# A two-layer graph network on one core: the second pass over the adjacency put in one written order, a third chunk of nodes summed by lists, and the nodes' own scores moved into layer 1

## The chip, the cores and the metric

The kernel runs on one core of a Trainium2 chip. TensorE (PE) multiplies matrices, VectorE (DVE) and ScalarE (ACT) work on elements, GpSimd (POOL) issues the indirect gathers here, SyncE (SP) issues most plain DMA transfers, and ACT issues a few. The metric is the device time of one execution in microseconds (us). The profile is of one further execution of the same program.

## The reference, cut to what matters

There are 3327 nodes with 512 features. `adj` is square, mostly zero, with non-zero weights from 0.05 to 1; the probability of an edge falls with the node numbers, so the first nodes (the hubs) have most edges. Cut from the reference:

```
# layer 0
h = relu(layernorm(x))
x = x + adj @ (relu(adj @ (h @ W1) + b1) @ W2) + b2        # W1: 512x128, W2: 128x512
# layer 1
h = relu(layernorm(x))
attn_a = sigmoid(concat([adj @ h, h]) @ Wa.T + ba)          # attn_b likewise with Wb, bb
hs = h @ W_sa
scores = (hs @ a_left)[:, None] + (hs @ a_right)[None, :]
e = where(adj != 0, exp(-leaky_relu(scores, 0.01)), 0)
x_a = (e / (sum(e, axis=1) + 1e-5)) @ hs
x_b = adj @ (h @ W_gcnb) + b_gcnb
x = x + sigmoid(attn_a * x_a + attn_b * x_b)
```

So layer 0 multiplies by `adj` twice, and layer 1 needs for every node the sum of its neighbours' rows of h, once weighted by `adj` and once by `e`. For every node it also needs a left score, a right score, and two logits from the node's own row (the part of Wa and Wb that meets h itself).

## The kernel before, in words

The nodes are padded to 3328 and cut into 26 blocks of 128. `adjT` is the transposed adjacency in DRAM. A chunk is 512 of its columns (one 256 wide); an adj tile is 128 rows by one chunk, 256 KB. All products are in float32, and each takes two passes of PE. The framework that the kernel is written in puts the semaphores in and plans the order of each engine's instructions by priority and readiness in its own model; `queued(...)` and `tc.issue_after(...)` put an instruction behind another one on the same engine, and `tc.high_priority()` moves work forward.

**Pass 1** (lines 541 to 596). Seven chunks from the last columns to the first. For each chunk and each block j, SP loads an adj tile (line 271, eight buffers), PE adds `u[j]` times the tile into `acc_u` (line 568; u is h @ W1, made beside the first chunk, line 333), and DVE takes for each row the maximum over each group of 32 columns (`most`, line 572). From these maxima DVE and PE make lists (lines 452 to 532): for a block of 128 nodes and each group of 32 columns, which rows of `adjT` are non-zero there. `list_rooms` gives each block its room, in steps of 64 rows per group: 0 for block 0, then 8, 7, 6, 5, 5, six times 4, then 3. For the blocks in `OWN` one more step holds the block's own diagonal part, which needs no list. POOL gathers the listed pieces of `adjT` into `ae` (line 166), paced by PE. ACT stores `g`, the relu of the sums, and between chunks loads weights and the columns of block 0 (`a_hub`, five pieces).

**Pass 2** (lines 806 to 860). The product `adj @ g`. For all nodes but the last two chunks it is dense: five chunks, 26 tiles each, line 825. For the last two chunks (blocks 18 to 25, `LISTED = 2`) the rows of g are gathered by list (`g_row`, line 166) and multiplied with the pieces in `ae` (`acc_s`, line 784, 64x32 pieces, four side by side). Each finished chunk gives a generator, `make_h1`, which is stepped between the dense products: for each block it loads x, adds b2, multiplies by W2 (`px`, line 663), adds (line 666), stores x1, normalises (`bn_stats`, `Sqrt`, line 234 to 244), takes the right and left score (line 623), the own logits (line 630, of the blocks that are neither in `OWN` nor in `LATE`), and stores the row of h (line 637). At the end of a chunk PE transposes the left scores (`pl`, line 687). Also stepped here are `make_e_hub` (the masked exponentials of block 0, lines 249 to 256) and `add_hubs` (block 0's two sums over all 26 blocks, `acc_hub`, line 709), and further gathers of `ae`. How often each is stepped is in conditions on the loop counters and in the table `SUMS`.

**Layer 1** (lines 914 to 1138). Block 0 has its sums already. The blocks 25 down to 1 follow. For each: POOL gathers the listed rows of h (`hr` or `rows`, line 166), DVE and ACT make the masked exponentials (`attend`), PE adds the rows by `adj` and by `e` (`sums`, line 981), transposes the result (`turn`, line 995; DVE copies it out, line 1010), multiplies by the weights (`weigh`, lines 1035 and 1042) and adds up the exponentials (`add_up`, line 1018); `finish` (lines 875 to 900) combines these and SP stores the output. In PE's order one round is: weigh an earlier block, turn the block before, add up, sums of this block. For a block in `OWN` its own rows of h are loaded (`h_own`, line 935, three buffers) and its own logits are made here; for the three blocks in `LATE` they are made at the start of layer 1.

Of the kernel before, what the change touches and what calls it, by code (L numbers as in the profile page):

```python
# [18 lines left out]
P = 128  # L19
# [9 lines left out]
LISTED = 2  # L29
LN_EPS = 1e-5  # L30
SUM_EPS = 1e-5
# [7 lines left out]
LATE = 10, 11, 16  # L39

OWN = 1, 6, 7, 8, 12, 13, 14, 15, 17, 18


def list_rooms(n_blocks):

    rooms = [0, 8, 7, 6, 5, 5] + 6 * [4]
    return (rooms + n_blocks * [3])[:n_blocks]
# [3 lines left out]
def kernel(  # L51
# [29 lines left out]
    made_order = []  # L81
    for k, c in enumerate(dense_chunks):
        for c0, w in (c, *listed_chunks[k : k + 1]):
            made_order += range(c0 // P, (c0 + w) // P)
# [3 lines left out]
    extra = [int(i in OWN) for i in range(NB)]  # L88
# [29 lines left out]
    bab_row = kept([P, 2], "bab_row")  # L118
    w_own = kept([P, 2, D], "w_own")
# [20 lines left out]
    def segments(i):  # L140

        r = rooms[i] + extra[i]
        n = -(-r // SEG)
        cuts = [-(-r * k // n) for k in range(n + 1)]
        return list(zip(cuts, cuts[1:]))
# [50 lines left out]
    def load_own(i):  # L196

        n = segments(i)[0][1]
        for h in range(2):
            rows = slice(i * P + h * HALF, i * P + (h + 1) * HALF)  # L200
            nc.scalar.dma_start(
                ae[i][h * HALF : (h + 1) * HALF, 0 : n + 1 : n, :GW],
                adjT[rows, rows].rearrange("j (q i) -> j q i", i=GW),
            )
# [41 lines left out]

    def masked_exp(e, adj):
# [11 lines left out]
    with (  # L259
        tc.tile_pool(name="l0", bufs=1) as l0,  # L260
        tc.tile_pool(name="l0w", bufs=2) as l0w,
        tc.tile_pool(name="adjp", bufs=8) as adjp,
    ):

        def load_adj(j, c, name, n=1):

            c0, w = c
            t = adjp.tile([P, CW], F32, tag="adj", name=f"{name}_{c0}_{j}")
# [17 lines left out]
        HUB_LOADS = 5  # L286

        def load_hub(k):
            rows = slice(k * NB // HUB_LOADS * P, (k + 1) * NB // HUB_LOADS * P)
            nc.scalar.dma_start(  # L290
                a_hub[:, k * NB // HUB_LOADS : (k + 1) * NB // HUB_LOADS, :],
                adjT[rows, :P].rearrange("(j p) i -> p j i", p=P),
            )

        def load_weights():
# [3 lines left out]
            nc.scalar.dma_start(w_own, w_self.partition_broadcast(P))  # L299
            nc.scalar.dma_start(bab_row, b_ab.partition_broadcast(P))  # L300
# [73 lines left out]
        def make_constants():  # L374
# [36 lines left out]
            for r in sorted(set(rooms[1:])):  # L411
                i0, n = rooms.index(r), rooms.count(r)
# [9 lines left out]
                )  # L422
            yield
# [9 lines left out]
        def make_lists(nth, most):  # L433
# [10 lines left out]
            for b in range(w // P):  # L444
                if extra[c0 // P + b]:
                    groups = slice(b * NQ, (b + 1) * NQ)
                    own = flag[:, groups, c0 // P + b]
                    nc.vector.tensor_tensor(own, own, apart, ALU.mult)

# [99 lines left out]
        for n, c in enumerate(back):  # L549
            c0, w = c  # L550
            acc = bank(psA, f"acc_u_{c0}")
            per = CW // w
            most = l0w.tile([P, MG, NB], F32, tag="most", name=f"most_{c0}")
            for j in range(NB):
# [9 lines left out]
                if j % per == 0:  # L564
                    with queued(x_loaded[min(j + 4, NB - 1)] if n == 0 else None):
                        tile_a = load_adj(j, c, "a1", per)
                a = tile_a[:, j % per, :]
                added = nc.tensor.matmul(  # L568
                    acc[:, :w], u[j], a[:, :w], start=(j == 0), stop=(j == NB - 1)
                )  # L570
                with queued(scaled[min(j + 3, NB - 1)] if n == 0 else None):
                    nc.vector.tensor_reduce(  # L572
                        most[:, : w // GW, j], a[:, :w].rearrange("p (b i) -> p b i", i=GW),
                        axis=AX.X, op=ALU.max, apply_absolute_value=True,
                    )
# [11 lines left out]
            with tc.issue_after(chunk_end.ins):  # L587
                if n == 1:
                    load_weights()
                if 0 < n <= HUB_LOADS:  # L590
                    load_hub(n - 1)
                for i in OWN:
                    if n and c0 <= i * P < c0 + w:
                        load_own(i)
# [24 lines left out]
        acc_hub = [bank(psA, f"acc_hub_{k}") for k in range(2)]  # L619

# [6 lines left out]
        def own_logits(i, h, junk):  # L627

            for s in range(2):
# [692 lines left out]
```

## Time and profile before

| | us |
|---|---|
| three runs, median | 825.4 (823.3 to 828.0) |
| profiled execution | 834.5 |
| its span on the core | 832.8 |
| PE busy | 735.6 (88%) |
| DVE busy | 506.0 (61%) |
| POOL busy | 461.1 (55%) |
| ACT busy | 194.5 (23%) |

185.1 MB went through DMA, 222 GB/s over the span. The stages, by the first and last instructions in the trace: pass 1 to 236 us, dense products and the hubs' products to 469, the first blocks of layer 1 to 490, then one block after another.

In the rows of the profile, a group is a line of the kernel, an engine, an operation and its tiles, with count and mean time. The chain is the work that ended last, followed back: each piece has a start, a length, and an engine with a line, or what was waited for. "Another core or an unknown queue" is a wait whose releaser the trace does not show; on one core it is no other core. "Issue" is time in which an engine waited for nothing that is shown. The granted clock is the share of full clock that PE had.

### The profile page before, as it was taken

The numbers are of one execution on the slowest core, as the hardware profiler recorded it, in microseconds if no ns is written. First come the engines' busy times: TensorE is split into PE (matmuls) and PEld (weight loads), VectorE is DVE, ScalarE is ACT, GpSimd is POOL, SyncE is SP. The second block draws the span as 40 slices with busy tenths as digits, with TensorE's granted clock in tenths as the row PEclk, the third lists the DMA queues.
The fourth block names the chain that finished last, engine by engine and source line by source line (L and its number), as shares of the span: only waits on it lengthen the run. The fifth ranks groups of instructions, "written<-read, shape, count | busy, mean of one in ns | idle before, by whom it ended". The sixth has DMA issues, their size and how long they took to land.

```text
span 832.8 us, 11907 instructions
## 1 busy us (share of the span) xinstructions
PE 735.6 (88%) x3595; PEld 404.5 (49%) x3595; DVE 506.0 (61%) x1625; ACT 194.5 (23%) x402; POOL 461.1 (55%) x490
## 2 busy tenths in 40 slices
PE   9999888989899771999899749967999999999995
PEld 7774333444543220444355236633656655665554
DVE  7778868898860611798987225523665557553552
ACT  7770000000000110354544002211212222221121
POOL 2201756766657776534456766674657666767500
PEclk9999989999999875999999969996999999999999
DMA  8788988988878844789994755664667877767510
GB/s 271 245 287 259 326 246 242 293 272 246 232 232 284 262 132 134 240 279 312 327 314 135 241 150 145 199 185 115 195 211 244 255 206 233 240 205 234 178 51 29
DMA packets 104889, 185.08 MB, mean 222 GB/s; under 512 B 18401, under 2 KB 35441, under 8 KB 104818
## 3 DMA queue, kind: packets, MB, share of 16 engines
q1 hardware_dynamic: 66544, 113.43, 41.8%
q0 software_dynamic: 23264, 57.64, 24.3%
q10 hardware_dynamic: 15010, 13.18, 4.9%
q8 instruction: 30, 0.49, 0.2%
q14 instruction: 41, 0.34, 0.1%
HBM read 162.29 MB, written 22.26 MB: 222 GB/s over the span
## 4 chain that ended last, share of the span: by engine, by line
PE 72%; DVE 7%; issue 6%; another core or an unknown queue 6%; DMA 5%; ACT 2%; POOL 1%; SPq 1%; DVEq 0%; ACTq 0%; POOLq 0%
PE acc_u L568 17%; PE acc L981 12%; PE p_b L1035 11%; PE p_a L1042 10%; PE acc_g L825 8%; PE pu L333 3%; PE ptt L995 3%; DMA a<-in_adjT_dram 2%; PE acc_hub L709 2%; PE px L663 2%; PE pt L325 1%; DMA xb<-in_x_dram 1%; PE acc_s L784 1%; DMA hr<-h_rows,row_h 1%
## 5 line engine op out<-in xcount | busy, mean ns | idle before, releaser
L166 POOL DMA_INDIRECT ae<-in_adjT_dram,row_a x194 | 202.6, 1044 | 181.8 <-DVE past L519 54.3
L568 PE MATMUL acc_u<-a,rows 128*128 128x512 f32 (+1 forms) x364 | 161.0, 583 | 0.5 <-DMA a<-in_adjT_dram 0.5
L166 POOL DMA_INDIRECT hr<-h_rows,row_h x120 | 122.7, 1022 | 62.5 <-issue 27.4
L825 PE MATMUL acc_g<-a,g 128*128 128x512 f32 (+1 forms) x260 | 117.1, 584 | 7.2 <-DMA a<-in_adjT_dram 6.8
L572 DVE TENSOR_REDUCE most<-a 128x16 f32<-128x512 f32 (+1 forms) x182 | 112.3, 638 | 11.6 <-issue 6.3
L1035 PE MATMUL p_b<-W_g_sb,tyT 128*128 128x257 f32 x416 | 99.3, 391 | 15.8 <-DVE tyT L1010 15.3
L1035 PEld LDWEIGHTS p_b<-W_g_sb,tyT 128*128 128x128 f32 x416 | 77.8, 192 | 46.5 <-DVE tyT L1010 15.6
L166 POOL DMA_INDIRECT rows<-h_rows,row_h x74 | 75.1, 1015 | 44.3 <-PE acc L981 20.9
L568 PEld LDWEIGHTS acc_u<-a,rows 128*128 128x128 f32 x364 | 67.2, 195 | 58.8 <-issue 56.0
L1042 PE MATMUL p_a<-W_sa_sb,tyT 128*128 128x512 f32 (+2 forms) x216 | 94.2, 577 | 0.2
L1010 DVE COPY tyT<-ptt 128x512 f32<-128x512 f32 x51 | 34.8, 685 | 87.0 <-PE p_a L1042 31.7
L825 PEld LDWEIGHTS acc_g<-a,g 128*128 128x128 f32 x260 | 50.0, 200 | 58.5 <-issue 44.9
L981 PE MATMUL acc<-hr,ae 64*64 64x512 f32 x480 | 68.3, 614 | 4.4 <-issue 4.0
L166 POOL DMA_INDIRECT g_row<-g_rows,row_h x48 | 49.0, 1021 | 20.9 <-issue 13.4
L1042 PEld LDWEIGHTS p_a<-W_sa_sb,tyT 128*128 128x128 f32 x216 | 40.7, 189 | 38.8 <-issue 36.9
L884 ACT ACTIVATE f<-f 128x2 f32<-128x2 f32 x26 | 5.3, 203 | 192.4 <-DVE f L883 97.2
L981 PEld LDWEIGHTS acc<-hr,ae 64*64 64x64 f32 x480 | 27.6, 136 | 33.6 <-issue 33.0
L343 ACT ACTIVATE gT<-acc_u,b_col 128x512 f32<-128x512 f32 (+1 forms) x7 | 4.6, 656 | 163.8 <-DMA a<-in_adjT_dram 90.9
L663 PE MATMUL px<-W_sb,sT 128*128 128x512 f32 x52 | 26.7, 650 | 15.4 <-ACT sT L799 12.0
L666 DVE TENSOR_TENSOR xb<-px,xb 128x512 f32<-128x512 f32 x26 | 17.3, 682 | 36.6 <-PE px L663 28.5
L981 PE MATMUL acc<-rows,ae 64*64 64x512 f32 x296 | 37.1, 593 | 2.5 <-issue 2.3
L623 DVE SCALAR_TENSOR_TENSOR junk<-rows,w_rows 128x512 bf16<-128x512 f32 x52 | 35.6, 684 | 3.2 <-ACT rows L244 1.1
(159 smaller groups left out, 945.2 us busy)
## 6 DMA issues: line engine op xcount, KB each, us to landing
a<-in_adjT_dram SPq DMA_DIRECT2D x286, 256.0 KB
h_rows<-rows SPq DMA_DIRECT2D x26, 260.0 KB
x<-in_x_dram SPq DMA_DIRECT2D x26, 256.0 KB
xb<-in_x_dram SPq DMA_DIRECT2D x26, 256.0 KB
x<-xb ACTq DMA_DIRECT2D x26, 256.0 KB
x1b<-x SPq DMA_DIRECT2D x26, 256.0 KB
out_dram<-va SPq DMA_DIRECT2D x25, 256.0 KB
ae<-in_adjT_dram,row_a POOLq DMA_INDIRECT x194
```

What stands on the lines that cost most here:

```text
L166: return nc.gpsimd.indirect_dma_start(out=dst, out_offset=None, in_=table, in_offset=bass.IndirectOffsetOnAxis(ap=rows, axis=0), bounds_ch ...
L333: nc.tensor.matmul(pu[:, :HID], hT[:, k, :], W1_sb[:, k, :], start=(k == 0), stop=(k == KD - 1))
L568: added = nc.tensor.matmul(acc[:, :w], u[j], a[:, :w], start=(j == 0), stop=(j == NB - 1))
L572: nc.vector.tensor_reduce(most[:, : w // GW, j], a[:, :w].rearrange("p (b i) -> p b i", i=GW), axis=AX.X, op=ALU.max, apply_absolute_value ...
L623: return nc.vector.scalar_tensor_tensor(junk, h, 1.0, w_rows[:, s, :], op0=ALU.mult, op1=ALU.mult, accum_out=into)
L663: last_row[2] = nc.tensor.matmul(px, sT[:, b * P : (b + 1) * P], W2_sb, start=True, stop=True)
L825: added = nc.tensor.matmul(acc[:, :w], g[j], a[:, n % per, :], start=(n == 0), stop=(n == NB - 1))
L981: added = nc.tensor.matmul(taken[i]["acc"][h][q * HALF : (q + 1) * HALF, :], both[half_p, q * n + k, :], taken[i][k0][k][half_p, q, :D], s ...
L995: moved = nc.tensor.transpose(pt[:, k * P : (k + 1) * P], ty[h][:, k * P : (k + 1) * P], ident)
L1010: last = nc.vector.tensor_copy(dst, src)
L1035: nc.tensor.matmul(p_b[n][:, :WH], tyT[:, k, 0, :], W_g_sb[:, k, n * WH : (n + 1) * WH], start=(k == 0), stop=(k == KD - 1),)
L1042: last = nc.tensor.matmul(p_a[:, c0:c1], tyT[:, k, 1, :], W_sa_sb[:, k, c0:c1], start=(k == 0), stop=(k == KD - 1),)
```

## The change

1. Third chunk by lists: `LISTED` is 3, so blocks 14 to 25 are summed by lists in pass 2, and the dense chunks are four (three of 512 and one of 256).
2. One written order for pass 2: the list `PLAN` names each step (d a dense product, s a list block, t the end of a listed chunk, x a block's row, l a transposition of left scores, h a hub product, e the exponentials of the hubs, a a gather of adj pieces), and every PE instruction is put behind the one named before it (`behind_pe`). `MADE` gives the order in which the chunks' rows are made.
3. A row in pass 2: the sum of x1 comes with its addition, the squares, the logarithm and the exponential are taken on ACT (`ln_relu_by_sum`), with one activation table loaded ahead for the whole pass. Only the right score is taken for every block, the left one for block 0 and blocks 22 to 25 (`early`).
4. Layer 1: every block's row is loaded a block ahead (`load_row`), DVE takes the left score (where not early) and the own logits (`own_scores`), PE transposes the left score (`turn_score`) between `add_up` and the next sums. `LATE` is gone; `w_own` and `bab_row` are loaded behind pass 2.
5. adj in pieces of two tiles (512 KB) with six buffers; maxima are taken over both tiles at once except in the first chunk.
6. Block 0's columns are loaded once, as part of the last chunk of pass 1 (in pieces of eight blocks, by SP), and used again in pass 2; products of that chunk are split into block 0's columns and the rest (`product`).
7. Blocks 9, 21 and 24 (`TOP`) have two steps without lists, their own and the 64 first rows of `adjT`, and one step less in lists; a block of five steps is taken in one segment.

```diff
-LISTED = 2
+LISTED = 3
+MADE = "dldlldd"
+PLAN = """
+d25 s1 d3 x1 d3 x1 s1 d2 l1 x1 d1 s1 d2 x1 e2 d5 s1 d2 t1 d2 x1 d2 s1 x1 e2 d6 x1 s1 d3 x1 e2
+d4 s1 d2 x1 l1 h1 s1 x1 e2 h1 t1 h1 a1 h1 d1 a1 d1 x1 a1 h1 s1 h1 x1 a1 e2 h2 a1 d2 a1 d1 s1
...
+d2 a1 h2 x1 a1 h2 a1 x1 h1 a1 h2 a1 h2
+"""
-LATE = 10, 11, 16
-
-OWN = 1, 6, 7, 8, 12, 13, 14, 15, 17, 18
+TOP = 9, 21, 24
+
+OWN = TOP + (1, 6, 7, 8, 12, 13, 14, 15, 17, 18)
...
-    rooms = [0, 8, 7, 6, 5, 5] + 6 * [4]
-    return (rooms + n_blocks * [3])[:n_blocks]
+    rooms = [0, 8, 7, 6, 5, 5, 4, 4, 4, 3, 4, 4] + n_blocks * [3]
+    rooms[21] = rooms[24] = 2
+    return rooms[:n_blocks]
...
-    extra = [int(i in OWN) for i in range(NB)]
+    extra = [int(i in OWN) + int(i in TOP) for i in range(NB)]
...
-        n = -(-r // SEG)
+        n = -(-r // SEG) - (r == SEG + 1)
...
+    def ln_relu_by_sum(dst, src, ln):
+
+        nc.vector.tensor_scalar(ln[:, 1:2], ln[:, 0:1], -1.0 / D, None, op0=ALU.mult)
+        nc.scalar.activation(dst, src, AF.Square, bias=ln[:, 1:2], accum_out=ln[:, 2:3])
+        nc.scalar.activation(ln[:, 3:4], ln[:, 2:3], AF.Ln, bias=eps, scale=1.0 / D)
+        nc.scalar.activation(ln[:, 4:5], ln[:, 3:4], AF.Exp, scale=-0.5)
+        nc.vector.tensor_tensor(ln[:, 0:1], ln[:, 1:2], ln[:, 4:5], ALU.mult)
+        return nc.scalar.activation(dst, src, AF.Relu, bias=ln[:, 0:1], scale=ln[:, 4:5])
...
-        tc.tile_pool(name="adjp", bufs=8) as adjp,
+        tc.tile_pool(name="adjp", bufs=6) as adjp,
...
-            t = adjp.tile([P, CW], F32, tag="adj", name=f"{name}_{c0}_{j}")
+            t = adjp.tile([P, 2 * CW], F32, tag="adj", name=f"{name}_{c0}_{j}")
...
+        def product(acc, w, own, j, a, start, stop):
+
+            hub = w - a.shape[-1]
+            if hub:
+                nc.tensor.matmul(acc[:, :hub], own, a_hub[:, j, :], start=start, stop=False)
+            return nc.tensor.matmul(
+                acc[:, hub:w], own, a, start=start and not hub, stop=stop
             )
...
+            hub = 0 if c0 else P
+            per = 2 * CW // (w - hub)
...
+                        if hub:
+                            load_hub(j, some)
+                        tile_a = load_adj(j, (c0 + hub, w - hub), "a1", some)
...
+                both = some if hub else 2 if n else 1
...
+        with queued(chunk_end):
+            nc.scalar.preload_act_table_set("natural_log_exp_and_others")
...
+        def make_row():
+
+            i = next(made)
+            load_next()
+            x1 = xs.pop(i)
+            assert place[i] - NR < len(e_added)
+            with tc.high_priority():
+                px = bank(psB, f"px_{i}")
+                with behind_pe():
+                    on_pe[0] = last_row[2] = nc.tensor.matmul(
+                        px, sTs.pop(i), W2_sb, start=True, stop=True
+                    )
+                ln = l0w.tile([P, 5], F32, tag="ln5", name=f"ln_b{i}", bufs=3)
+                nc.vector.scalar_tensor_tensor(
+                    x1, px, 1.0, x1, op0=ALU.mult, op1=ALU.add, accum_out=ln[:, 0:1]
+                )
+                nc.scalar.dma_start(x1_dram[i], x1)
+                h = made_row(i)
+                last_row[0] = ln_relu_by_sum(h[:, :D], x1, ln)
+                score(i, h[:, :D], 1, h[:, D : D + 1])
+            last_row[1] = last_row[0]
+            if i in early:
+                last_row[1] = score(i, made_row(i)[:, :D], 0, node[i][:, 0:1])
...
+            while len(unstored) > (0 if place[i] > NB - 7 else 3):
+                store_row(unstored.pop(0))
...
+        plan = [(w[0], int(w[1:])) for w in PLAN.split()]
+        for n in range(4):
+            next(dense)
         gather_g(GR)
...
+        for what, n in plan:
+            for _ in range(n):
+                does[what]()
...
+    with queued(last_row[0]):
+        nc.scalar.preload_act_table(AF.Tanh)
...
+        def load_row(i):
+
+            h_own[i] = h = spw.tile([P, ROW], F32, tag="h_own", name=f"h_own_{i}", bufs=3)
+            nc.sync.dma_start(h, h_dram[i * P : (i + 1) * P, :])
+
+        def own_scores(i):
+
+            if i not in s_left:
+                nc.vector.scalar_tensor_tensor(
+                    junk, h_own[i][:, :D], 1.0, w_left, op0=ALU.mult, op1=ALU.mult,
+                    accum_out=node[i][:, 0:1],
+                )
+            own_logits(i, h_own[i], junk)
+
+        def turn_score(i):
...
+            turned = nc.tensor.transpose(pl[:, :P], node[i][:, 0:1].to_broadcast([P, P]), ident)
+            s_left[i] = spw.tile([P, 2 * GW], F32, tag="s_left", name=f"s_left_{i}", bufs=3)
+            for h in range(2):
+                half_p = slice(h * HALF, (h + 1) * HALF)
+                nc.scalar.copy(s_left[i][half_p], pl[half_p, h * HALF : (h + 1) * HALF])
...
         for i in range(NB - 2, 1, -1):
             with queued(*held):
+                load_row(i - 1)
                 for seg in segments(i):
                     made = attend(i, seg)
-            if i == NB - 2:
-                own_of(LATE[2], made[0])
+                own_scores(i - 1)
...
+            with queued(added):
+                added = turn_score(i - 1) or added
```

## The prediction

> **What bounds the kernel now.** I read the page first: the TensorE (PE) row, the granted clock and the chain that ended last.
>
> ```profile
> span 832.8 us, 11907 instructions
> PE 735.6 (88%) x3595; PEld 404.5 (49%) x3595; DVE 506.0 (61%) x1625; ACT 194.5 (23%) x402; POOL 461.1 (55%) x490
> PE   9999888989899771999899749967999999999995
> PEclk9999989999999875999999969996999999999999
> PE 72%; DVE 7%; issue 6%; another core or an unknown queue 6%; DMA 5%; ACT 2%; POOL 1%; SPq 1%; DVEq 0%; ACTq 0%; POOLq 0%
> ```
>
> PE carries 72% of the chain, so the time is PE's work plus the holes in it, and the holes sit in a few slices. Next the stretches view, cut at the stages (start:end, length, busy time of each engine, granted clock, DMA share, GB/s):
>
> ```profile
> 66.00:236.00 170.00, 151.53 (x723) 73.62 (x723) 144.36 (x381) 3.91 (x6) 103.64 (x101) 0.95 0.86 263
> 236.00:340.00 104.00, 72.77 (x260) 30.42 (x260) 34.21 (x102) 9.44 (x20) 67.25 (x65) 0.79 0.65 210
> 340.00:447.00 107.00, 101.34 (x371) 50.14 (x370) 90.74 (x309) 52.61 (x89) 54.68 (x51) 1.00 0.85 281
> 447.00:469.00 22.00, 21.85 (x53) 9.43 (x51) 11.19 (x44) 5.39 (x13) 14.51 (x15) 1.00 0.76 257
> 469.00:490.00 21.00, 3.83 (x32) 1.68 (x32) 3.54 (x11) 2.55 (x5) 14.07 (x15) 0.69 0.51 143
> 490.00:833.00 343.00, 319.97 (x1766) 189.93 (x1766) 173.07 (x619) 73.26 (x163) 195.28 (x192) 0.96 0.60 182
> ```
>
> 66 to 236 is pass 1 behind its first chunk, 236 to 469 pass 2 with the hubs' products, 469 to 490 the way into layer 1, 490 to 833 layer 1. The worst stretch is 236 to 340: PE idle for 31 us and at 0.79 of its clock for the rest. From 340 on VectorE (DVE) is at 85% and DMA at 0.85. Then the chain in order of time (start, length, what):
>
> ```profile
> 265.11 9.13 another core or an unknown queue
> ...
> 308.65 8.78 another core or an unknown queue
> 318.65 13.65 another core or an unknown queue
> ...
> 364.41 1.00 PE acc_s L784 x30
> ...
> 416.39 2.58 PE acc_hub L709 x6
> ...
> 462.19 6.11 DMA hr<-h_rows,row_h
> ...
> 473.05 16.46 another core or an unknown queue
> ```
>
> L709 and L784 give prices at full clock: 0.43 us for a 512-wide pass (a product is two, 0.86 us) and 0.033 us for a pass of a list sum. The four unknown waits are 48 us; who waits there is ScalarE (ACT), DVE or SP, on PE. Last SP's waits, which layer 1 will need:
>
> ```profile
> SPq L900 <- DVE va L899: 263.8, 21, 45.5
> ```
>
> **The change, part by part.** I sum against the profiled execution, 834.5 us (span 832.8), which is 9.1 above the median of the runs, 825.4; I take 9.1 off at the end.
>
> *Pass 1, 66 to 236.* It loses 170 - 151.5 = 18.5 us to idle PE and 151.5 x 0.05 = 7.6 to the clock, 26 in all. The stock of adj grows from 8 tiles to 6 x 2, of which 10 are ahead: 10 x 0.86 = 8.6 us of PE against 7 x 0.86 = 6.0, so a DVE burst of list making (the chain shows 4.7 us of waiting for a tile after one) is more often covered. 130 maxima become 65; by the two widths (676 ns at 512, 408 at 256) the fixed part is 0.14 us, so DVE gives up 9 us of 144, and the hubs' columns are not loaded twice (1.7 MB of 45). Splitting chunk 0 into 128 + 128 costs PE nothing: four 128-wide passes take 0.44 us (eight in pass 1's u products, 0.89), two 256-wide ones 0.43. Against it: the first tile of a pair waits for 256 KB more, 1 us at 263 GB/s, at six stalls 6 us. Bounds -26 and +6; I take -11, as DMA was at 0.86 already.
>
> *Pass 2, 236 to 469 (233 us).* PE's work at full clock is 104 x 0.86 + 26 x 0.43 dense, 26 x 0.86 x1, 52 x 0.86 hub, 200 x 0.033 list sums and 4 of transposes: 178 us, so 55 us are holes and slow clock. Removed: 26 products of 512 (-22.4) and 21 left-score transposes (-2.3, at 0.11). Added: 4 blocks by lists and a step each for blocks 21 and 24, 144 passes (+4.8) and 4 transposes (+0.4). New work 158.5 us. The other queues: DMA moved 104 x 210 + 107 x 281 + 22 x 257 GB/s = 57.6 MB; less a chunk (6.8) and the hub columns (1.7), plus 20 g gathers (1.3), less 24 adj gathers (0.4): 50.0 MB. POOL issues 4 + 68 + 43 = 115 gathers, each 1.0 us and 0.3 of issue: 150 us, and its list sums stand in the plan about where 1.3 us each puts the landings. DVE loses per row the statistics (0.68 + 0.16 + two of 0.15) and for 21 rows a score (0.77), and all 13 pairs of own logits (1.53); this is what filled DVE from 340 on. ACT gains a square, a log and an exp for each row (some 1.3 us x 26), beside 166 us of slack, and drops nearly all table loads here (18 at 1.28 us, several in a row's own chain). So PE, DMA and POOL all want 150 to 180 us. At 281 GB/s, the rate of 340 to 447, where PE was busy for 101.3 of 107 us, 50.0 MB take 178 us; with the start 180. Ends: 158.5 (PE never waits, -74) and 238 (the 210 GB/s of 236 to 340, +5). I take 180, the row nearest to a filled queue: -53.
>
> The Trainium skill, "DMA: Bandwidth & Descriptors", section Specifications, gives a core about 358 GB/s of HBM. By that, 50 MB are 140 us, PE would be the bound and this term -74; no slice of this trace passes 327.
>
> *Order.* PE's instructions of pass 2 now stand in one list, so a late one holds all behind it: a list sum whose gathers are late holds the dense products, and with them the tiles and SP's next loads. That is inside the 180.
>
> *Into layer 1.* Behind the last row 25 hub products (21.5 us) covered store, gather and attention; the list leaves 16 (13.8), so PE idles up to 8 us more, less about 3 as the last row stands alone: +5. Before the turn of block 0, DVE now makes own logits of three blocks instead of one, 2 x 1.53 = +3, w_own's load lying beside the gathers (6.1 us). The unknown 16.5 us there: nothing shows its cause, so -15 to 0, and I take -7. Sum +1.
>
> *Layer 1.* Blocks 9, 21, 24 sum one step more: 3 x 0.87 = +2.6. 21 transposes: +2.3. Each stands in PE's order between the row sums and the next block's sums, so it waits for the row load and DVE's score. SP issues that load behind the last block's output store, which waits for DVE (263.8 us of SP's waits are of this kind). In one block of before, 600.5 to 612, the store goes out 2.5 us after p_b begins and the transpose would be due 8.0 us after; load at 3.4, landing 3.4 us later (the first x load) to 6.1 (the first gather), score 0.8: ready at 7.6 to 10.3, so 0 to 2.3 us each, 0 to 48 in all. I take 0.3, as the row is traced a block ahead: +6. DVE's 37 us more and 4.2 MB more of rows lie in a stage where DVE is at 50% and DMA at 0.60. POOL has 6 row gathers fewer but some 18 more of adj left over, +16 us in 343 at 57% busy; if it is late, the big blocks pay, as at 750. Of the 23 us idle I take off 3 (-16 to 0). Sum +8.
>
> Sum: -11 - 53 + 1 + 8 = -55; 834.5 - 55 = 779.5, less 9.1 is **770 us**.
>
> The clock, by rows: after the holes of 236 to 340 the clock is 0.79, and at 469 to 490 0.69, so a hole costs again behind it. The Trainium skill, "TensorE: Matmul & The Clock Gate", section HAM oscillation, says that idling over about 3.4 us halves the clock; the trace agrees (0.50 from 320 to 330, where PE stood). It speaks against the change where the cover shrinks: an 8 us hole into layer 1 would by it cost an estimated 2 us more, with the sum at 772.
>
> **Rivals.**
> *All holes close:* pass 1 -20, pass 2 -70, into layer 1 -8, layer 1 +6: -92, 733; I place it at 735. For it: each of the unknown waits stands in code that is rewritten. Against: three queues at 85% and more.
> *Only PE's work goes:* the holes of pass 2 are DMA's and POOL's and stay: 233 - 19.5 = 213.5 us (50 MB at 234 GB/s, between the rows), pass 1 -5, the rest +9: -15.5, **810**. For it: 236 to 340 ran at 210 GB/s with POOL full; 20 more gathers stand there. Against: 340 to 447.
> *Slower:* the left-score transposes hold PE in every block of layer 1. It is a loss from 61/21 = 2.9 us each, a row landing 6.7 us after its issue; at 3.5 us the sum is -61 + 73 = +12, **837**. For it: SP's order above. Against: before, rows were loaded 12 us ahead of use (598.1 to 610.2), and p_b and p_a give 7.3 us of cover.
> *No change:* gains and that wait cancel, 825.
>
> **Chances and range.** Forecast 0.52 (its own range 752 to 792), all holes 0.10, only the work 0.20, no change 0.05, slower 0.13. A measurement tells 0.5%, 4 us, from no change. Faster 0.82, same 0.05, slower 0.13. The range 737 to 829 leaves out half of the best case and the slower one.
>
> **What would show it.** Pass 2 from its first dense product to its last hub product: 180 us right, over 205 wrong. GB/s there near 280. PE's clock at 1.00 where it was 0.79. DVE under 70% in pass 2, no table loads between rows. Pass 1's six later chunks in 150 to 165 us. In layer 1 PE idle before the pl transposes: under 0.5 us each right, 3 us the slower rival. The forecast falls if the list sums wait on POOL or if the rows' x loads starve behind adj pieces.

## The result, and the profile after

The changed kernel takes 882.6 us (median of four executions, 879.6 to 884.1), the kernel before beside it 826.7 (four, 823.3 to 834.4): a ratio of 1.066, 95% interval 1.058 to 1.074. It is 6.6% slower; the forecast was 770.

The sets of runs fall into two groups, slowed sets (the measurement above is one), in which the kernel before takes 827 to 832 us, and free sets, in which the same kernel takes 733 to 735 us; one chip number occurs in both groups, so it is not the chip as such, and times are compared within a set or by their ratio to the kernel before of their set.

The page after, to be read against the five lines shown of before:

```profile
span 877.6 us, 11970 instructions
PE 754.0 (86%) x3799; PEld 409.3 (47%) x3799; DVE 483.4 (55%) x1500; ACT 203.1 (23%) x490; POOL 474.3 (54%) x516
PE   7999889899876978823899559989998999899995
PEclk9999979899895999955899669999999999999999
PE 68%; issue 12%; DVE 5%; POOL 4%; DMA 4%; another core or an unknown queue 3%; ACT 2%; SPq 0%; ACTq 0%; POOLq 0%; DVEq 0%
```

PE has as many holes as before, in part at new places, and 12% of the chain is "issue", time in which an engine waited for nothing that is shown (6% before). The stretches, cut at the stages of this kernel (start:end, length, busy time of PE, weight loads, DVE, ACT, POOL, granted clock, DMA share, GB/s):

```profile
72.00:239.00 167.00, 151.22 (x755) 76.56 (x755) 140.10 (x314) 3.97 (x7) 101.75 (x100) 0.93 0.78 242
239.00:360.00 121.00, 97.75 (x489) 49.92 (x488) 38.89 (x129) 27.76 (x70) 75.38 (x74) 0.87 0.74 237
360.00:420.00 60.00, 25.15 (x91) 8.72 (x89) 8.35 (x29) 4.83 (x13) 43.25 (x43) 0.60 0.26 70
420.00:488.00 68.00, 66.74 (x231) 34.44 (x231) 42.56 (x154) 34.66 (x90) 3.00 (x3) 0.98 0.64 209
488.00:516.00 28.00, 7.83 (x36) 2.64 (x34) 7.12 (x24) 2.37 (x5) 19.95 (x20) 0.62 0.74 234
516.00:877.00 361.00, 338.98 (x1811) 186.64 (x1811) 197.70 (x693) 82.27 (x200) 218.13 (x206) 0.98 0.61 181
```

The third row is new: for 60 us PE is busy for 25, at 0.60 of its clock, DVE and ACT hardly work, DMA moves 70 GB/s at a share of 0.26, and POOL alone is busy, with 43 instructions that take 43 us. The chain in that stretch, and the two unknown waits further on:

```profile
385.34 2.10 DMA ae<-in_adjT_dram,row_a
387.44 1.33 issue
389.15 1.04 issue
390.55 2.44 issue
...
503.94 11.21 another core or an unknown queue
...
578.51 10.40 another core or an unknown queue
```

The same place on PE's timeline (start, duration, engine, line, operation, tiles, count, idle time before):

```profile
379.68 0.37 PE L823 MATMUL acc_s<-g_row,ae 64*32 64x128 f32 x1 [1.76 <-issue]
381.79 0.37 PE L823 MATMUL acc_s<-g_row,ae 64*32 64x128 f32 x1 [1.74 <-issue]
...
403.48 1.01 PE L747 MATMUL acc_hub<-rows,e_hub 128*128 128x512 f32 x1 [1.78 <-issue]
406.29 1.01 PE L747 MATMUL acc_hub<-rows,e_hub 128*128 128x512 f32 x1 [1.80 <-issue]
```

and on POOL's:

```profile
380.14 0.99 POOL L175 DMA_INDIRECT ae<-in_adjT_dram,row_a  x1 [0.30 <-issue]
381.44 1.00 POOL L175 DMA_INDIRECT ae<-in_adjT_dram,row_a  x1 [0.30 <-issue]
382.75 0.99 POOL L175 DMA_INDIRECT ae<-in_adjT_dram,row_a  x1 [0.30 <-issue]
```

PE's instructions, weight loads included, stand 0.70, 1.40, 2.10 or 2.80 us apart, whatever their size and though the profile shows nothing that they wait for. POOL issues a gather every 1.30 us. From 354.7 to 415.2 us 47 gathers, the last 43 of them the plan's `a` steps, follow each other without a pause over 0.3 us; PE slows at 368 and is at its normal pace from 419 on. Signals are late too: the product px of 362.8 ended at 363.8, and DVE's addition that reads it began at 376.2.

The stages of both profiled executions, by the start of the first matmul of the next one (us); pass 2 ends with the start of the last hub product, and layer 1 is counted from its first product by the weights. Cut in this way pass 2 of before takes 236.1 us, where the prediction cut at 236 us and had 233:

| | before | after | difference |
|---|---|---|---|
| first chunk of pass 1 done | 65.8 | 72.1 | +6.3 |
| its six later chunks | 166.4 | 166.6 | +0.2 |
| pass 2, to the last hub product | 236.1 | 249.8 | +13.7 |
| into layer 1, to its first product by the weights | 22.0 | 27.4 | +5.4 |
| layer 1 | 342.4 | 361.7 | +19.3 |

With this pattern in mind the trace of before reads differently. Its runs of 20 and more gathers, by the times of the first and the last issue, go from 240.1 to 270.7 us (24 gathers), 302.4 to 327.1 (20), 455.6 to 485.7 (24) and 538.9 to 568.9 (24), and its unknown waits lie at 265.1 to 274.2, 308.7 to 332.3 (two, 1 us apart) and 473.1 to 489.5; a step of layer 1 that takes 30.9 us instead of 10.8 ends at 577. Beside the first of these runs PE kept its pace, and only its signals were late: the last of three products px ended at 265.0 us, and DVE's addition that reads it began at 272.1. In the changed kernel the runs end at 278, 415, 512 and 586, and the slow stretches or unknown waits at 284, 419, 515 and 589. This is a correlation; the experiments test it.

Last, the wait of SP for the last output store, which was 263.8 us in all, is

```profile
SPq L959 <- DVE va L958: 78.9, 9, 14.3
```

while SP now also waits 93.4 us to load a block's row into a free buffer (line 986); none of this is on the chain.

### The profile page after: what moved, and what is told of

Its sections match the earlier page's. It is cut to its first block, busy times and chain, and to the rows that moved or that the text cites. A ratio compares the mean times of both kernels' runs of the same rounds, so it can differ in the third digit from the quotient of the medians.

```text
span 877.6 us, 11970 instructions
## 1 busy us (share of the span) xinstructions
PE 754.0 (86%) x3799; PEld 409.3 (47%) x3799; DVE 483.4 (55%) x1500; ACT 203.1 (23%) x490; POOL 474.3 (54%) x516
## 4 chain that ended last, share of the span: by engine, by line
PE 68%; issue 12%; DVE 5%; POOL 4%; DMA 4%; another core or an unknown queue 3%; ACT 2%; SPq 0%; ACTq 0%; POOLq 0%; DVEq 0%
PE acc_u L317 14%; PE acc L1070 12%; PE p_b L1124 10%; PE p_a L1131 9%; PE acc_g L317 6%; PE acc_hub L747 4%; PE ptt L1084 2%; POOL g_row L175 2%; PE pu L357 2%; PE px L694 2%; POOL ae L175 2%; DVE most L609 2%; DMA x<-in_x_dram 1%; PE p_list L541 1%
## 5 line engine op out<-in xcount | busy, mean ns | idle before, releaser
L175 POOL DMA_INDIRECT ae<-in_adjT_dram,row_a x188 | 192.5, 1024 | 130.8 <-PE acc_u L317 76.2
L609 DVE TENSOR_REDUCE most<-a 128x32 f32<-128x1024 f32 (+2 forms) x95 | 99.2, 1053 | 8.9 <-DMA a<-in_adjT_dram 7.3
L317 PE MATMUL acc_g<-a,g 128*128 128x512 f32 (+2 forms) x208 | 91.0, 555 | 10.2 <-issue 10.2
L175 POOL DMA_INDIRECT g_row<-g_rows,row_h x68 | 69.1, 1016 | 43.0 <-PE acc_s L823 19.1
L698 DVE SCALAR_TENSOR_TENSOR xb<-px,xb 128x512 f32<-128x512 f32 x26 | 17.9, 687 | 100.9 <-PE px L694 84.6
L317 PEld LDWEIGHTS acc_g<-a,g 128*128 128x128 f32 x208 | 39.8, 203 | 41.8 <-issue 40.0
L1070 PEld LDWEIGHTS acc<-hr,ae 64*64 64x64 f32 x480 | 22.8, 134 | 46.6 <-issue 44.1
L261 ACT ACTIVATE rows<-xb,ln_b 128x512 f32<-128x512 f32 x26 | 18.8, 722 | 101.6 <-DVE e_hub L276 47.2
L1006 ACT COPY s_left<-pl 64x64 f32<-64x64 f32 x42 | 8.7, 206 | 120.9 <-PE acc L1070 49.8
L922 DVE SCALAR_TENSOR_TENSOR a_hub<-h_own,w_own 128x512 f32<-128x512 f32 x52 | 35.5, 682 | 0.1
```

The costliest lines, as they stand in the source:

```text
L175: return nc.gpsimd.indirect_dma_start(out=dst, out_offset=None, in_=table, in_offset=bass.IndirectOffsetOnAxis(ap=rows, axis=0), bounds_ch ...
L261: nc.scalar.activation(dst, src, AF.Square, bias=ln[:, 1:2], accum_out=ln[:, 2:3])
L317: return nc.tensor.matmul(acc[:, hub:w], own, a, start=start and not hub, stop=stop)
L609: nc.vector.tensor_reduce(most[:, to, j : j + both], part.rearrange("p k (b i) -> p b k i", i=GW), axis=AX.X, op=ALU.max, apply_absolute_v ...
L698: nc.vector.scalar_tensor_tensor(x1, px, 1.0, x1, op0=ALU.mult, op1=ALU.add, accum_out=ln[:, 0:1])
L922: nc.vector.scalar_tensor_tensor(junk, h[:, :D], 1.0, w_own[:, s, :], op0=ALU.mult, op1=ALU.mult, accum_out=node[i][:, 1 + s : 2 + s],)
```

## The experiments

The theories: **A**, a long run of gathers on POOL, one behind the other without a pause, slows PE and the signals between engines. **B**, the written order makes PE stand behind late list sums. **C**, the pieces of two tiles starve PE or the x loads. Later **D** (A depends on the condition of the machine), **E** (the hubs' columns delay the start) and **F** (buffers for x).

### First set: the fetches paced, replaced, the order dropped, one-tile pieces

The fetches of the plan's `a` steps, each behind the PE product named before it:

```
             with queued(g_last[0]):
-                next(columns, None)
+                gather_behind(on_pe[0])
```

> The 43 fetches of adj groups in pass 2 (the plan's a steps), which POOL issued one behind the other from 360 to 416 us, each wait for the PE product that stands before them in the plan; PE's own order is unchanged. Theory A (a long run of gathers on POOL slows PE, whose instructions then come 0.7 to 2.8 us apart though none of them waits for data): the stretch 368 to 418 us, where PE was busy 12 of 50 us, needs about 15 us, so 35 to 45 us go: 838 to 848 us. Theory B (PE stands because the written order puts late list sums ahead): the list sums' own gathers are not touched, no more than 5 us go: 877 to 883. Theory C (pieces of two tiles starve PE): no change.

The same fetches replaced by two iotas each (an iota fills a tile with numbers and starts no DMA; the groups of adj stay zero, so this kernel leaves out what they would add):

```
+                        if idle:
+                            for _ in range(2):
+                                stand_in = nc.gpsimd.iota(idle[0], ...)
+                            yield stand_in
+                            continue
                         yield gather(
```

> The same 43 fetches are replaced by 43 pairs of iotas on POOL (about 1.1 us a pair, no DMA); their groups of adj stay zero in layer 1, so this work is left out. If it is POOL being occupied that slows the others: 875 to 885, as the changed kernel. If it is the writing and running of the gathers' descriptors: the hole at 368 to 418 us closes as in the run before, 835 to 850 us, and POOL's run of iotas shows PE at full rate beside it. Theory B (order): 875 to 885.

The order dropped:

```
         def behind_pe():
-            return queued(on_pe[0])
+            return queued()
```

> The one written order of PE is dropped: each PE instruction of pass 2 goes where the planner puts it, all else as changed. Theory A (gathers): the runs of gathers on POOL remain, so the holes at 256 to 281 and 368 to 418 us remain: 870 to 890 us. Theory B (the order holds PE behind late list sums): 35 to 50 us go, 833 to 848 us.

One-tile pieces:

```
-        tc.tile_pool(name="adjp", bufs=6) as adjp,
+        tc.tile_pool(name="adjp", bufs=8) as adjp,
...
-            t = adjp.tile([P, 2 * CW], F32, ...)
+            t = adjp.tile([P, CW], F32, ...)
...
-            per = 2 * CW // (w - hub)
+            per = CW // (w - hub)
...
-                both = some if hub else 2 if n else 1
+                both = some
```

> adj comes again in pieces of one tile (of two where a chunk is 256 wide) with eight buffers, in both passes; DVE again makes one maximum a tile; the hubs' columns are still loaded once and pass 2 keeps its order. Theory C (the larger pieces hold the x loads and the tiles back): the first chunk ends at 66 us again, 6 to 10 us are gained there; pass 1 loses some 5 us by DVE's 65 more maxima: 872 to 890 us. Theories A and B: the holes of pass 2 stand, within 10 us of 882.

Measured, beside a kernel before of 733.5 us, in a free set:

| | us | ratio to before | 95% interval |
|---|---|---|---|
| fetches behind PE | 741.8 | 1.011 | 1.002 to 1.020 |
| fetches replaced | 742.2 | 1.013 | 1.004 to 1.022 |
| no order | 737.9 | 1.007 | 1.003 to 1.011 |
| one-tile pieces | 751.4 | 1.026 | 1.017 to 1.034 |

Every expectation in absolute times missed, since none of the slowing was there. In the run without an order POOL issued 194 and then 225 gathers in a row, with no pause over 0.35 us, while PE kept its normal pace. Two things follow all the same. The written order is no source of a large loss in such a set: without it the kernel is still 0.7% above the one before. And theory C falls for the start: with one-tile pieces the first chunk ended even later, at 74.4 us. The chain of that run names what was in the way (start, length, what):

```profile
13.76 6.58 DMA a_hub<-in_adjT_dram
20.35 2.95 DMA a<-in_adjT_dram
23.31 0.81 ACT h L255
```

### Second set: both kernels as they stand

> The changed kernel as it stands. The four experiments so far ran on a chip on which the kernel before takes 733.5 us and not 826.7, and all of them lay within 0.7 to 2.6% of it. Theory D (on the chip of the first measurement PE was slowed during long runs of gathers on POOL, on this chip it is not, and the change lengthens those runs): the changed kernel is within 1% of the kernel before here, 733 to 742 us, with PE busy over 9 of 10 in every slice of pass 2 except its ends. Theory B (the written order itself costs 50 us): 780 or more on any chip.

> The kernel before as it stands, for its profile on the same chip. Theory D: the 24 gathers in a row at the start of pass 2 are there as in the first profile, but the waits of 9, 9, 14 and 16 us for PE's semaphore at 265, 309, 319 and 473 us and the 30.9 us step of layer 1 are not, and pass 2 takes 233 less some 45 to 60 us. If instead these waits stand: the time lies near 826.

This was a slowed set: 880.6 us against 831.9, a ratio of 1.062 (1.057 to 1.068); the kernel before, run as an experiment, 832.0. The first measurement repeats, with the same signs: PE's instructions 0.70 us apart or a multiple of it at 260 to 284 and 371 to 425 us, and, in the kernel before, unknown waits of 9.5 us at 261 and 15.3 us at 461. The expectation of theory D for this set (within 1%) missed, as the condition had changed; that the condition goes with the chip, as its text has it, fails on the chip number that occurs with both.

### Third set: the fetches paced and replaced again, and all spread

> The edit of the first experiment again (the 43 fetches of adj groups in pass 2 each wait for a PE product), beside a kernel before of about 830 us. Theory A (on this chip a run of more than some 10 us of gathers on POOL makes PE's instructions come 0.7 us apart or more): the run of 47 gathers at 356 to 417 us is broken up, the slow stretch 371 to 425 us goes, 835 to 850 us against 880.6. Theory B (the written order holds PE behind list sums): 875 to 885. Should the kernel before take about 733 us here, nothing is slowed and the run says only that the edit is worth under 1%.

> The edit of the second experiment again: 43 pairs of iotas in place of the 43 fetches, one behind the other, without a DMA; their adj groups stay zero, that work is left out. If POOL being busy is what slows PE: slow stretch as before, 870 to 885. If it is the gathers' descriptors or their transfers: 835 to 850, with PE at full rate beside iotas that run back to back for some 50 us.

For the third kernel the first edit, and:

```
-a1 h2 d1 a1 d1 x1 a1 e2 h2 ...
+a2 h2 d1 a2 d1 x1 a2 e2 h2 ...
...
                     if c == 0 and n < 4:
                         gather_behind(on_pe[0])
+                    if c * NB + n in (15, 28):
+                        gather_g(8, on_pe[0])
...
                 g_last[0] = gather(t, g_dram[:, :], row_h[:, f : f + 1], NP - 1)
+                if behind is not None:
+                    pace(g_last[0], behind)
+                    behind = None
...
-        gather_g(GR)
+        gather_g(8)
```

> The first edit, and: the 24 gathers of g rows at the start of pass 2 come in three lots of 8, the second and third each behind a PE product (the 16th and the 29th), and 17 more of the adj groups are fetched at the end of pass 2, so 23 instead of 40 are left for layer 1. Theory A, where the kernel before takes about 830: the slow stretches 261 to 284 and 371 to 425 go, and of those in layer 1 (581, 687, 718 us) one or two: 805 to 835. Theory B: 870 to 885. Where the kernel before takes about 733, all POOL work is hidden: 733 to 745.

A slowed set, kernel before 827.5 us:

| | us | ratio to before | 95% interval |
|---|---|---|---|
| fetches behind PE | 835.1 | 1.010 | 1.006 to 1.014 |
| fetches replaced | 833.2 | 1.013 | 1.004 to 1.022 |
| spread | 832.7 | 1.009 | 1.006 to 1.013 |

The first edit takes the changed kernel from 6.2% above the one before (second set) to 1.0%, some 45 us, as theory A had it. All of it lies in pass 2, which takes 204.2 us for 249.4 in the second set. PE's instructions and their order are the same in both, so theory B cannot give this. The stretches of that run, the first row nearly the one where the 47 stood in a row:

```profile
360.00:426.00 66.00, 62.56 (x282) 32.87 (x281) 42.63 (x147) 31.25 (x82) 37.70 (x37) 0.99 0.75 226
426.00:445.00 19.00, 19.00 (x46) 8.57 (x46) 9.08 (x36) 8.70 (x22) 12.89 (x13) 1.00 0.65 203
```

PE is busy for 62.6 of 66 us where it was for 25 of 60, at 0.99 of its clock, though POOL's gathers are still all there: 37 and 13 instructions of POOL in the two rows. The 43 fetches go from 361.6 to 437.6 us, one in 1.8 us on average, 18 of them after a pause of 0.7 us or more, and the longest row without such a pause is of 13, at the end. The same run holds its own comparison: the 25 gathers that stand unpaced from 248.9 to 281 us keep their slow stretch, and PE is busy for 12.5 of the 24 us from 260 to 284, at 0.61 of its clock. Replaced by iotas:

```profile
360.26 53.99 POOL L202 IOTA place_row<- 128x512 f16 x86
```

POOL is busy for 54 us without a pause, and the time is 833: a busy POOL does not slow PE; gathers do. Whether by what POOL does to start a transfer or by the transfers themselves is not separated, since the iotas have neither; that the DMA engines were full is ruled out by their share of 0.26 in the slow stretch.

The spread kernel took the slow stretch of layer 1 away in part (layer 1 from 363 us in the first run of this set to 341.5), but the 17 fetches more made a run of 59 gathers from 404 to 484 us, behind which the first rows of layer 1 stood: from the last hub product to the first product by the weights 44 us, against 27. In sum nothing. This run also bounds theory A: beside its first 40 us PE kept its pace, busy for 47.0 of the 50 us from 395 to 445. The gathers came more loosely there, 30 from 403.6 to 444.1 us, one in 1.40 us on average, as nine of them took 1.1 to 1.5 us instead of 1.0. So the length of a run is not the whole condition; whether the closeness of its gathers is the rest, and where a limit lies, no run tests. The stretch at 261 to 284 became one at 245 to 262 us, with POOL's run of 25 at one in 1.30 us cut to 16: shorter, not gone. The time is at the upper end of what was expected.

### Fourth set: the hubs' columns late

```
+        adj_loaded = [None]
...
-            nc.sync.dma_start(t, rows.rearrange("(k p) i -> p k i", p=P))
+            adj_loaded[0] = nc.sync.dma_start(t, rows.rearrange("(k p) i -> p k i", p=P))
...
                         if hub:
-                            load_hub(j, some)
+                            with queued(adj_loaded[0]):
+                                load_hub(j, some)
```

> The changed kernel with one thing moved: the hubs' columns (four loads, 1.7 MB), which the planner put at 8.8 us ahead of the first x loads, are issued in the last chunk of pass 1, each behind the adj piece before it. Theory E (these loads, not the larger pieces, hold the x loads back at the start): the first chunk ends at 66 us and not at 72, 5 to 8 us less: 873 to 877 where the kernel before takes about 830, about 733 where it takes 733. If the larger pieces do it: no change at the start, 878 to 883.

This and the third set's first edit, with the lots of g rows, but with the plan as it was:

> The edit of the run before this one, the adj groups of pass 2 each behind a PE product, and the 24 first gathers of g rows in three lots of 8. Theories A and E together: 45 us (first edit) and 6 us (hubs' columns) and 0 to 10 us (three lots): 820 to 830 where the kernel before takes about 830; 728 to 738 where it takes 733.

And to this:

```
-                if j % 4 if w == CW else j % 2:
+                if j % 2:
                     gather_behind(added)
```

> As the run before this one, and in pass 1 a gather after every second product (one in 1.7 us) and not after three of four (one in 1.15 us, less than the 1.30 us that one takes, so that runs of 16 to 19 arise). If it is the share of time without gathers that matters, a pause of 0.4 us after each, the slow stretch at 105 to 117 us goes and pass 1 gains 8 to 12 us, less what the some 10 gathers more cost later (10 x 1.3 us of POOL): 815 to 828. If only whole pauses of 2 us and more help: pass 1 stays slow, 825 to 840. Where the kernel before takes 733: 728 to 745.

A free set (kernel before 735.1): 739.7 (ratio 1.007, 1.004 to 1.011), 739.3 (1.005, 1.002 to 1.008) and 768.2 (1.044, 1.039 to 1.049), the first two 1 to 7 us above what was expected there, the last far off. The first chunk ends at 66.0 us with the hubs' columns late. What stood there is seen in SP's issues of the changed kernel as it was measured first:

```profile
8.38 0.43 SPq L291 DMA_DIRECT2D a<-in_adjT_dram  x1
8.86 4.66 SPq L307 DMA_DIRECT2D a_hub<-in_adjT_dram  x3
13.62 1.52 SPq L333 DMA_DIRECT2D x<-in_x_dram  x1
15.19 0.43 SPq L307 DMA_DIRECT2D a_hub<-in_adjT_dram  x1
```

The code asks for these columns in the last chunk of pass 1, at some 215 us; nothing holds them, so the planner issues them at 8.9 us, ahead of x. The last kernel left only 72 groups of adj fetched by 220 us; POOL then issued 204 gathers from 458 to 733 us with no pause over 0.35 us, and the two steps of layer 1 that begin at 678 and 706 us took 27.5 and 23.9 us. Its question, whether pauses of 0.4 us suffice, needs a slowed set and stays open.

### Fifth set: four kernels once more

> The changed kernel as it stands. Where the kernel before takes about 733: 740 to 748 (its edits so far took 737 to 742 there, and the hubs' columns cost 6 at the start). Where it takes about 830: 878 to 884.

> The kernel before, for its profile in this set. Where it takes about 733: pass 2 (first dense product to last hub product) 180 to 195 us, pass 1's six later chunks 150 to 157, layer 1 from its first product 315 to 325: the whole gain in pass 2 that the forecast counted on is then mostly gone from the start. Where it takes about 830: 227 to 237, 162 to 167, 342.

> The hubs' columns late, nothing else. Where the kernel before takes about 830: theory E 872 to 877, first chunk to end at 66 us. Where it takes 733: 737 to 742.

> The hubs' columns late, the adj groups of pass 2 behind PE products, the first 24 gathers of g rows in three lots of 8. Where the kernel before takes about 830: 820 to 832, the 45 and the 6 us together, and nothing or up to 8 for the lots. Where it takes 733: 737 to 742.

A free set again, kernel before 733.5 us: the changed kernel 745.3 (ratio 1.016, 1.011 to 1.022), the kernel before run as an experiment 732.6, hubs' columns late 739.1 (1.006, 1.002 to 1.010), with the spread 739.0 (1.009, 1.006 to 1.012); all four as expected in time, the kernel before a little faster in the later chunks of pass 1 and in layer 1 than was written. By these medians the columns cost 6.2 us. By stages of the profiled executions, 7 us go at the start and 5 come back in the later chunks, where the 1.7 MB now land, so one profile does not show where the 6 stay. What the free set is worth for the forecast is the pair of profiles without slowing. Before:

```profile
66.00:215.00 149.00, 141.79 (x710) 67.30 (x710) 139.49 (x373) 3.76 (x6) 101.27 (x99) 1.00 0.95 296
215.00:340.00 125.00, 120.10 (x512) 53.62 (x510) 88.83 (x288) 39.88 (x71) 93.17 (x87) 1.00 0.96 320
340.00:408.00 68.00, 64.54 (x182) 33.85 (x183) 50.59 (x174) 27.90 (x52) 48.76 (x44) 0.97 0.79 262
```

After:

```profile
73.00:222.00 149.00, 141.45 (x757) 71.55 (x757) 139.92 (x314) 3.91 (x6) 101.83 (x96) 0.99 0.85 269
222.00:343.00 121.00, 112.13 (x658) 56.98 (x656) 55.29 (x188) 39.17 (x101) 93.86 (x90) 0.97 0.90 294
343.00:398.00 55.00, 53.42 (x150) 28.76 (x150) 33.26 (x122) 28.16 (x72) 37.19 (x36) 0.97 0.67 215
```

In the kernel before PE is busy for 120 of the first 125 us of pass 2, at full clock: the 31 us of idle PE that the forecast meant to win are not part of the kernel's own structure, they come with the slowing. And beside the same 25 gathers, from 226 to 259 us here, PE of the changed kernel is busy for 33.0 of 33 us at full clock. By stages: first chunk 65.9 to 73.0 (+7.1), later chunks 149.4 to 148.6, pass 2 193.1 to 176.3 (-16.8), into layer 1 9.2 to 17.6 (+8.4), layer 1 311.7 to 323.0 (+11.3), together +9.2.

### Sixth set: more buffers for x

In these sets SP waits 38.3 us in pass 2 for x buffers whose row is still being stored (line, releaser, us in all, times, longest):

```profile
SPq L684 <- DMA x<-xb: 38.3, 12, 6.1
```

To take that wait away:

```
-        tc.tile_pool(name="adjp", bufs=6) as adjp,
+        tc.tile_pool(name="adjp", bufs=5) as adjp,
...
-                xs[i] = l0w.tile([P, D], F32, tag="x", name=f"xb_{i}", bufs=5)
+                xs[i] = l0w.tile([P, D], F32, tag="x", name=f"xb_{i}", bufs=7)
...
-        load_next()
-        load_next()
+        for _ in range(4):
+            load_next()
```

> As the run after this one, with seven buffers for the rows' x instead of five (four loaded ahead instead of two) and five for pieces of adj instead of six, so the same memory. Theory F (SP, waiting 38 us in pass 2 for stored rows to free the x buffers, holds the rows and the adj pieces queued behind it): pass 2 takes 163 to 170 us instead of 177, 726 to 734 where the kernel before takes 733; 810 to 825 where it takes about 830. If the sixth adj buffer is worth as much: 738 to 745 (830 to 838).

> Hubs' columns late, adj groups of pass 2 behind PE products, g rows in three lots. Where the kernel before takes about 733: 737 to 741, as twice before. Where it takes about 830: 820 to 832 by theories A and E.

A free set, kernel before 733.4 us: 745.7 (1.017, 1.014 to 1.021) with more x buffers and 741.9 (1.011, 1.008 to 1.014) without. The wait did not go:

```profile
SPq L684 <- DMA x<-xb: 39.0, 8, 9.8
```

Fewer waits, some longer, the same sum (39.7 in the run beside it), and pass 2 takes 182.2 us beside 178.6. As the wait that was to go stayed, the run does not show what it costs: theory F is not confirmed, and its price stays open. The rows' x are a suspect all the same. In the changed kernel of the fifth set 18% of the chain of pass 2 is x loads on their way and 11% stores of x1, against 9% and 2% in the kernel before; that is the sign "if the rows' x loads starve" of the prediction's last line. It can be worth hardly more than PE's idle time there, some 10 of 176 us. No changed version that was run beats the kernel before in either condition.

## Why the prediction was wrong, step by step

**The step that failed is pass 2: "I take 180 ... -53", with the order's cost "inside the 180".** In the measured condition pass 2 went from 236 to 250 us, +13.7. Within it, the term that was mis-sized is "POOL issues ... 115 gathers, each 1.0 us and 0.3 of issue: 150 us". It counted a gather as POOL's own time beside other work. In the slowed sets gathers that follow each other closely take PE's time as well, and the plan put the `a` steps behind POOL's own last gather only, where the kernel before put each of its fetches in pass 2 behind a PE product. That alone is 45 us (880.6 to 835.1 against kernels before of 831.9 and 827.5). Without it pass 2 takes 204 us, where the kernel before takes 226 and 236 us in its two slowed profiles, so even then only 22 to 32 of the 53 us come in a slowed set; the stretch beside the first 25 gathers is still in it.

**The cause of the holes was left open and their end was booked.** "The four unknown waits are 48 us", the text said, and of the last that "nothing shows its cause". The trace did show what stood beside each of them: a run of 20 to 24 gathers that had begun 6 to 25 us earlier. Laying the unknown waits on POOL's timeline would have suggested the rival that happened; the last line of the prediction named a wait of the list sums on POOL, which is a small part of it (POOL is 4% of the chain).

**Where nothing is slowed, the time of pass 2 comes out and the gain does not.** Pass 2 takes 176 us (forecast 180), at 270 GB/s on the whole (forecast near 280), DVE at 50% (under 70%). But there the kernel before needs only 193, so the gain is 17 us and not 53. That 176 is close to 180 is in part luck: the 180 rested on 281 GB/s as the rate at which DMA is full, and the kernel before moves 320 GB/s over 125 us of its pass 2 in the free set. What was counted rightly is the work: PE's busy time in pass 2 falls by 19 us (184.6 to 165.6), close to the 19.5 counted.

**Pass 1, -11.** The later chunks: +0.2 in the slowed pair, -0.8 in the free one; no gain of the larger stock or of the 65 maxima less is to be seen, though DVE's instructions on `most` take 8 to 10 us less, as counted (93.2 to 83.4 slowed, 91.1 to 83.3 free). And the prediction summed pass 1 from 66 us on, with the first chunk at nothing. It moved the hubs' columns on paper to where the code asks for them, and not to where a planner may put a load that waits for nothing: 6.3 us.

**Into layer 1, +1.** +5.4 slowed, +8.4 free. The hole in front of the first sums, put at +5, grew by 7.8 slowed and 7.7 free; the +3 for own logits is not to be seen, as in the free pair the products by the weights wait 0.3 us for DVE before and after. That 5 and 3 make 8 is luck. The -7 for the unknown wait came in part: it belongs to a run of gathers and went from 16.5 to 11.2 us. And the sums behind the longer hole ran at half the clock in the slowed pair, 5.3 us for 2.7.

**Layer 1, +8.** Free +11.3: a step with a left-score transpose takes 11.17 us for 10.81, 0.36 for each of 21 blocks, 7.6 in all (the text had 2.3 + 6), and three sums more, 2.6; the 3 us of idle time taken off did not come. Slowed +19.3: 40 groups of adj are fetched behind the last hub product instead of 20, and POOL has runs of 16 to 19 gathers there; beside them four steps take 18 to 21 us, where one step of before takes 30.9. The text saw "some 18 more of adj left over" and bounded it by POOL's busy time alone.

**The rivals.** None of them is what happened. The slower rival's mechanism is refuted. PE's idle time before the 21 left-score transposes of the changed kernel, by the view of their line (us, times), is

```profile
  issue: 1.2, 2
```

where it needed 2.9 us for each. "Only PE's work goes" was right in size for pass 2 only where nothing is slowed, and gave 810, since it too kept the holes' removal apart from their cause.

## What to carry to other kernels

Lay every wait "for an unknown queue" and every stretch of "issue" on the timelines of all engines before booking its end; what runs beside each of them is the first suspect. Count gathers on POOL twice: as POOL's time, and by the length of their runs, and pace each behind a product of PE, as one edited line did here for 45 us in a slowed set (in the free sets the kernel with it is 1.1% above the one before, without it 1.6%). A load that waits for nothing is issued where the planner likes it: name what it is to stand behind.

## What the runs showed of the hardware

- In the slowed sets, from some 6 to 25 us into a run of gathers that follow each other at 1.30 us, signals between engines come late, by up to 15 us (in the kernel before the transposes end at 475.0 us and DVE's copy of them begins at 489.5), and beside most such runs PE's instructions come 0.70 us apart or at multiples of it; it ends 2 to 8 us behind the run's last issue. 43 gathers at one in 1.8 us on average, in rows of at most 13 without a pause of 0.7 us, did not do it, nor 30 at one in 1.40 us, nor 54 us of iotas.
- In the free sets it does not occur at all: the kernel before issues 214 gathers there from 399.5 to 683.8 us with no pause over 0.6 us, and in layer 1 PE is busy for 302 of 311 us. The same program takes 733 us in these sets and 830 in the others; how much of the difference is such stretches was not added up. One chip number occurs with both; what sets the condition, and by what route gathers reach PE, no run here shows.
